# Half of the weight sums on GpSimd moved from the scan into the first products of layer 2, and the residual tiles' pools split anew

## The chip, the cores and the metric

The kernel runs on one core of a Trainium2 chip. The metric is the device time of the whole program in microseconds, median of several executions. Beside it there is one profiled execution, from which every duration below is taken. PE is TensorE, DVE is VectorE, ACT is ScalarE, POOL is GpSimd, SP is SyncE, whose queue issues most DMAs.

## What is computed

The input x is fp32, 1024 channels of 64 × 64 positions (1024 × 4096). Four layers are applied, each to a group-normalized copy, and each adds its result to x:

```python
x = x + L0_conv(gn(x))     # a scan convolution
x = x + W1 @ gn(x) + b1    # 1x1 convolution, 1024 -> 1024
x = x + L2_conv(gn(x))     # below
x = x + W3 @ gn(x) + b3    # 1x1 convolution, 1024 -> 1024
```

Layer 2, cut to what matters here:

```python
xz = silu(in_proj_w @ x + in_proj_b)          # 3072 x 4096
x_ssm, res, gate = split(xz, 3)               # WX, WR, WG below
xf = silu(depthwise_conv3(x_ssm) + dw_b)
perm = argsort(mobius_score)                  # an order of the 4096 tokens, for each of two heads
dt, B, C = split(dbc_w @ xf + dbc_b)          # 1 + 8 + 8 rows per head
y = selective_scan(xf[perm], softplus(dt)[perm], A, B[perm], C[perm], D)[inverse perm]
out = silu(out_proj_w @ (y * silu(gate) + res) + out_proj_b)   # WO below
```

## The kernel before, in words

**Matrices and products.** Six 1024 × 1024 matrices are multiplied with 1024 × 4096 data: W1, WX, WR, WG, WO, W3. W1, WX and WR run as a one-step fast product, 7 products of halves in place of 8 (`multiply`, L827, called by `run`, L898; columns go in four pairs of 512-column blocks). The right-hand sides of the seven are b21, b11, b22 and the combinations t1 to t4, made in `b_sets` (L786, the subtractions at L799 partly on DVE, partly on POOL) for the next pair while the present one is multiplied. WG, WO and W3 run at the end as a two-step product (`two_steps`, 7 × 7 = 49 products a job, 12 jobs); 9 of the 49 left-hand sides are blocks of the matrix, 40 are sums of blocks, which have to lie in DRAM (`s2_d`) before.

**The sums.** `sum_weights2` (L463) makes these 40 sums of one matrix, in chunks of `width` columns. A chunk loads 16 blocks into a tile of 7 × 4 × width per partition (four loads, L477), makes the inner sums with four POOL operations of 128 × 4·width (L479 and, inside `sub`, L470), stores three of the four block columns (L486), makes the outer sums in place with four POOL operations of 128 × 7·width (L490, L470), and stores four more (L497). Since the outer sums write over what the first stores read, they wait for these stores; the next chunk's loads wait for the last ones, as there is one tile. It is a generator: at each `yield` it hands over to the loop that advances it, and one advance is called a step here. Steps place the instructions in each engine's order; they are no waits in themselves.

**The stages.** Layer 0 takes the first 240 us, layer 1 up to 640. Sums for WR and WG are made in layer 1. From 640 to 1130 WX is multiplied (L1230 to L1262). For each output block the depthwise convolution follows, then turned rows are made: four 128-column pieces are turned on PE (L1086), copied by ACT (`l2xt`, three buffers, L1088), added into `acc` by POOL (L1094), and stored as token rows to `tok_d` by SP. `sort_on` advances the sort that gives `perm` in the same loop, by a written list of 14 numbers, one for each product of a pair.

From 1130 to 1645 the scan runs (L1302 to L1430) beside WR's products. An iteration k gathers the rows of the tokens of iteration k + 5 from `tok_d` in the order of perm (`gather`, L1310, an indirect DMA on POOL), turns rows (`turn_rows`, L1324 and L1325), makes the decay (DVE), `cross` (L1346), `weigh` (L1354 to L1359), `apply` (L1363), and scatters the result (`scatter`, L1372, also on POOL). `next_units` puts WR's products between. WR's results go through `rg` tiles: `put2b` (L1026) copies the first part out of PSUM by ACT, `add2b` adds the rest, `activate` applies silu and stores to `res_d`. Before the scan loop starts, `first` = 13 units of WR are put: eight beside the end of WX's stage, five after the first five gathers.

The same loop makes the sums for WO and then W3: one step an iteration, except where `given // 2 % 14 == 12`:

```python
sums = (None for m in (WO, W3) for _ in sum_weights2(m, ph, nc.sync, 64, lag=(1, None)))
...
                if given // 2 % 14 != 12:
                    next(sums, None)
```

With `lag=(1, None)` a chunk takes four steps: loads; two steps later the inner sums and, in the same step, the first stores; one step later the outer sums and the last stores; one step later the next chunk. Two matrices of eight chunks of width 64 make 64 steps.

**Pools.** `rg` tiles, one for each output block of a put, lie in two pools: `l2r` with four tiles, opened before WX's stage (L1017), and `l2r2` with six, opened after it in memory that WX's stage (`l2a` and its companions) has just left. The first six `rg` tiles of WR (for the products b21, b22 and t2) are made before `l2r2` is open, so all in `l2r`; from the seventh on (t3's first) the written rotation `[prg] * 6 + rg_pools * 4` holds, six tiles of `l2r2` and then four of `l2r`. `sort_pool` is on the right side of the memory and closes after WX's stage.

**Order.** In the loops concerned the order on DVE, PE, POOL and ACT is the written one (`manual_schedule`); SP's is that of the DMA calls.

Of the kernel before, what the change touches and what calls it, by code (L numbers as in the profile page):

```python
# [20 lines left out]
P = 128  # L21
# [73 lines left out]
def tile_net(ctx: ExitStack, tc: tile.TileContext, x, par_d, cst_d, w_d, w2_d, dbcw_d, out):  # L95
# [318 lines left out]
    def sort_on(quiet, n):  # L414


        while coming[0] is not None:
            was = coming[0]
            if was == "compare":
                if n == 0 or not quiet:  # L420
                    return
                n -= 1
            coming[0] = next(order, None)
            if was != "compare" or coming[0] != "compare":
                return
# [9 lines left out]
    def pause(n, first=None):  # L435
        yield first
        for _ in range(n - 1):
            yield
# [21 lines left out]
                dma.dma_start(d[:, at], w)  # L460
            yield

    def sum_weights2(m, pool, dma, width=P, lag=(0, 0)):  # L463

        eng = nc.gpsimd

        def sub(out, a, b):
            eng.tensor_tensor(out, a, b, ALU.subtract)  # L470

        for c in range(2 * QO // width):
            at = slice(c * width, (c + 1) * width)

            w = pool.tile([P, 7, 4, width], F32, tag="s2", name=f"s2_{m}_{c}", bufs=1)
            for i, block in ((0, 0), (1, 1), (2, 3), (5, 2)):
                dma.dma_start(w[:, i], w2_d[m - NW, 4 * block : 4 * block + 4, :, at].rearrange("j p e -> p j e"))  # L477
            yield from pause(1 + lag[0])
            eng.tensor_tensor(w[:, 3], w[:, 5], w[:, 2], ALU.add)  # L479
            sub(w[:, 5], w[:, 0], w[:, 5])  # L480
            sub(w[:, 4], w[:, 3], w[:, 0])
            sub(w[:, 6], w[:, 1], w[:, 4])
            if lag[1] is not None:
                yield from pause(1 + lag[1], True)
            for j, block in enumerate((0, 1, 3)):
                dma.dma_start(s2_d[m][3:, j, :, at].rearrange("i p e -> p i e"), w[:, 3:, block])  # L486
            if lag[1] is None:
                yield True
            a11, a12, a21, a22 = (w[:, :, j] for j in range(4))
            eng.tensor_tensor(a22, a21, a22, ALU.add)  # L490
            sub(a21, a11, a21)
            sub(a11, a22, a11)
            sub(a12, a12, a11)
            if lag[1] is not None:
                yield from pause(1 + lag[1], True)
            for j, v in ((3, a22), (4, a11), (5, a21), (6, a12)):
                dma.dma_start(s2_d[m][:, j, :, at].rearrange("i p e -> p i e"), v)  # L497
            yield

# [474 lines left out]
    def forget(pairs):  # L976
        for pair in pairs:
# [7 lines left out]
    norm2, last = {}, NP * NG * 7 - 1  # L985
    FIRST, SECOND = ([row * KH + g * OG + o for row in range(2) for o in range(OG)] for g in range(NG))
    sums = (busy for f in (sum_weights(WR, sum1, nc.scalar, lag=(1, 1)),
                               sum_weights2(WG, sum1, nc.scalar, lag=(2, 1))) for busy in f)
    with tc.manual_schedule(engines={E_.DVE, E_.PE, E_.Pool, E_.Activation}):
        for i, _ in enumerate(pointwise("l1", W1, "b1", [3, 2] + EARLY, x0_d, x1_d)):  # L990
            busy = next(sums, None) if i % 14 < 13 else None
# [22 lines left out]

    rg_pool = tc.tile_pool(name="l2r", bufs=4)  # L1017
    rg_pools = [rg_pool.__enter__()]
    part, silus = {}, []

    def put2b(m, o, nb, ps):
# [19 lines left out]
    with tc.tile_pool(name="l2a", bufs=2) as pa, tc.tile_pool(name="l2a2", bufs=1) as pa2, \  # L1041
# [184 lines left out]
        with tc.manual_schedule(engines={E_.DVE, E_.PE, E_.Pool, E_.Activation}):  # L1226
            nc.sync.dma_start(both[:, :, P:], dbcw_d)
            nc.gpsimd.tensor_copy(both[:, :, :P], ident.unsqueeze(1).to_broadcast([P, CT, P]))
            nc.gpsimd.memset(row, 0.0)
            ends, i, chain = iter(()), -1, None  # L1230
            for half in run(EARLY + LATE, [WX], normed(norm2), put2a, add2a, before2,
                            last_eng=nc.vector, fine=True, tell=True, begun=begun):
                if len(norm2) < CT:
                    n = len(SECOND)
                    if chain is None:
                        moments("gn2b", SECOND, range(2, 4), mv2)
                        chain = norm_steps("gn2b", mv2[:, 0, :n], mv2[:, 1, :n], n, finer=True)
                        turns = 0
                    turns += 1
                    if turns < 3:  # L1240
                        next(chain), next(chain)
                    else:
                        columns(SECOND, finish_of(chain), norm2)
                if half:
                    if coming[0] == "take":
                        sort_on(True, 0)
                    if due3:
                        turn(*due3.pop(0))
                elif half is False:
                    turned = bool(due3)  # L1250
                    follow()
                    follow_on()
                if half is not None:
                    continue
                i += 1
                if i > 14 and i % 14 == 4:
                    ends = finish(i // 14 - 1)
                next(ends, None)
                if coming[0] != "turn" or not turned:
                    sort_on(True, (0, 0, 0, 1, 3, 1, 0, 2, 0, 2, 3, 3, 0, 0)[i % 14])  # L1260
            while coming[0] is not None:
                sort_on(True, 1)  # L1262

            forget(EARLY)
            units = run([3, 2] + EARLY, [WR], normed(norm2), put2b, add2b, before2, fine=True, B=last_B[0])
            total, first, given = NP * 2 * NG * 7, 13, 0

            def next_units(upto):
                nonlocal given
                if given < upto:  # L1270
                    given += 1
                    next(units, None)

            while ready or due or due2 or due3:
                follow()
                next_units(8)
                next_units(8)
                follow_on()
                next_units(8)
                activate(len(silus))  # L1280
            spare = []
            for i in range(2):
                w = pa.tile([P, 2 + 2 * FB], F32, tag="xs", name=f"row{i}", bufs=4)[:, : 3 * HEADS * NF2]
                nc.gpsimd.memset(w, 0.0)
                spare.append(w.rearrange("p (b h c) -> p b h c", b=3, h=HEADS))
            for _ in finish(NP - 1):
                pass

    sort_pool.__exit__(None, None, None)

    with tc.tile_pool(name="l2g", bufs=8) as pgat, tc.tile_pool(name="l2b", bufs=2) as pb, tc.tile_pool(name="l2r2", bufs=6) as prg, tc.tile_pool(name="l2h", bufs=1) as ph, \
            tc.tile_pool(name="ps2b", bufs=1, space=PSUM) as psb:
        rg_pools[:] = [prg] * 6 + rg_pools * 4
        G2 = [ph.tile([P, P], F32, name=f"G{i}") for i in range(2)]
        B2 = [(ph.tile([MW, P], F32R, name=f"bts{i}"), ph.tile([MW, S, LC], F32R, name=f"cd{i}"))
              for i in range(2)]  # L1300
# [73 lines left out]
                in_=y, in_offset=None,  # L1374
            )

        sums = (None for m in (WO, W3) for _ in sum_weights2(m, ph, nc.sync, 64, lag=(1, None)))

# [461 lines left out]
```

## Time and profile before

| what | us |
|---|---|
| median of 3 executions | 2714.77 (2713.36 to 2717.06) |
| the profiled execution | 2715.32 |
| its span (first to last instruction) | 2713.4 |
| PE busy in the span | 2578.7 |
| POOL busy in the span | 1218.4 |
| layer 0, 0 to 240: PE busy | 163.43 |
| layer 1, 240 to 640: PE busy | 391.81 |
| scan stage, 1130 to 1645: PE, DVE, ACT, POOL busy | 485.95, 365.97, 330.00, 314.98 |

A span is what the profiler sees between the first and the last instruction; the time of the execution has 1.9 us around it. Where PE's clock column is below 1, its matmuls run slower though they count as busy. A hole before an instruction is put down to what released it last.

### The profile page before, as it was taken

The numbers are of one execution on the slowest core, as the hardware profiler recorded it, in microseconds if no ns is written. First come the engines' busy times: TensorE is split into PE (matmuls) and PEld (weight loads), VectorE is DVE, ScalarE is ACT, GpSimd is POOL, SyncE is SP. The second block draws the span as 40 slices with busy tenths as digits, with TensorE's granted clock in tenths as the row PEclk, the third lists the DMA queues.
The fourth block names the chain that finished last, engine by engine and source line by source line (L and its number), as shares of the span: only waits on it lengthen the run. The fifth ranks groups of instructions, "written<-read, shape, count | busy, mean of one in ns | idle before, by whom it ended". The sixth has DMA issues, their size and how long they took to land.

```text
span 2713.4 us, 30641 instructions
## 1 busy us (share of the span) xinstructions
PE 2578.7 (95%) x9520; PEld 1718.4 (63%) x9520; DVE 1817.8 (67%) x3870; ACT 1086.8 (40%) x1839; POOL 1218.4 (45%) x1100
## 2 busy tenths in 40 slices
PE   4788999999999999999999999999999999899999
PEld 3664444444555555444454447888888888788887
DVE  6996856655555644477677766577585676877777
ACT  4783110103656555476767554332243133311220
POOL 4154123232122120257575655576565566554544
PEclk9898999999999999999999999999999999999999
DMA  7245467546443373587877975889899898788896
GB/s 288 107 166 201 148 218 266 186 124 231 125 150 105 111 170 110 165 257 231 240 234 235 314 222 172 240 242 297 226 294 274 240 304 232 249 295 296 301 320 218
DMA packets 422741, 597.22 MB, mean 220 GB/s; under 512 B 141972, under 2 KB 210707, under 8 KB 419508
## 3 DMA queue, kind: packets, MB, share of 16 engines
q1 hardware_dynamic: 298020, 367.89, 42.4%
q10 hardware_dynamic: 91456, 136.33, 14.4%
q0 software_dynamic: 33104, 91.04, 13.1%
q8 instruction: 77, 1.26, 0.2%
q14 instruction: 84, 0.69, 0.1%
HBM read 435.10 MB, written 160.05 MB: 219 GB/s over the span
## 4 chain that ended last, share of the span: by engine, by line
PE 45%; DMA 6%; DVE 2%; ACT 2%; POOL 1%; SPq 1%; issue 1%; ACTq 0%; POOLq 0%; DVEq 0%
PE mm L841 7%; PE q_P6P L1716 5%; PE q_P5P L1716 5%; PE q_P7P L1716 5%; PE q_P4P L1716 5%; PE q_P2P L1716 5%; PE q_P3P L1716 5%; PE q_P1P L1716 4%; PE py L1363 1%; DMA s_d<-s 1%; DMA x_x_b<-x_d 1%; POOL s L470 1%; DMA s<-in_w_dram 1%; DMA g<-tok_d,src 1%; DMA x_x_Z<-x_d 1%
## 5 line engine op out<-in xcount | busy, mean ns | idle before, releaser
L841 PE MATMUL mm<-t,w 128*128 128x512 f32 x1536 | 694.4, 603 | 7.9 <-POOL t L799 4.1
L841 PE MATMUL mm<-b,w 128*128 128x512 f32 x1152 | 515.1, 598 | 4.0 <-ACT b L945 2.9
L841 PEld LDWEIGHTS mm<-t,w 128*128 128x128 f32 x1536 | 289.7, 193 | 337.0 <-issue 318.4
L841 PEld LDWEIGHTS mm<-b,w 128*128 128x128 f32 x1152 | 216.4, 192 | 253.0 <-issue 240.7
L1067 DVE SCALAR_TENSOR_TENSOR cvp<-xs,par,cvp 128x512 f32<-128x512 f32 x128 | 95.3, 754 | 75.5 <-ACT cvp L1064 73.3
L1685 ACT COPY qQ<-q_P5P 128x512 f32<-128x512 f32 x48 | 28.1, 586 | 293.7 <-PE q_P5P L1716 276.8
L1094 POOL TENSOR_TENSOR acc<-l2xt,acc 128x136 f32<-128x136 f32 x56 | 29.0, 519 | 235.5 <-ACT l2xt L1088 234.6
L470 POOL TENSOR_TENSOR s<-s 128x256 f32<-128x256 f32 (+3 forms) x120 | 130.1, 1091 | 7.9
L1118 DVE TENSOR_TENSOR xs<-mm,xs 128x512 f32<-128x512 f32 x64 | 41.8, 685 | 124.2 <-PE mm L841 124.2
L1366 ACT COPY g<-py 8x512 f32<-8x512 f32 x146 | 83.9, 574 | 95.0 <-PE py L1363 92.6
L960 DVE SCALAR_TENSOR_TENSOR image<-mm,par,image 128x512 f32<-128x512 f32 x64 | 47.0, 746 | 98.0 <-PE mm L841 98.0
L1372 POOL DMA_INDIRECT y_rows<-g,dst x74 | 73.5, 993 | 66.5 <-ACT g L1368 34.1
L1086 PEld LDWEIGHTS l2pt<-both,cv 128*128 128x128 f32 x512 | 76.5, 190 | 32.6 <-issue 23.9
L799 POOL TENSOR_TENSOR t<-t,b 128x512 f32<-128x512 f32 x40 | 56.0, 1425 | 91.2 <-DVE t L799 60.7
L1310 POOL DMA_INDIRECT g<-tok_d,src x74 | 72.1, 974 | 52.9 <-PE pr L1325 18.0
L1484 ACT ACTIVATE qb<-x_x_b,gn_bias,gn_r_r 128x512 f32<-128x512 f32 x64 | 48.8, 807 | 113.6 <-DMA wq_P4P<-s_d 32.3
L1354 DVE TENSOR_TENSOR E<-E,pg 128x512 f32<-128x512 f32 x74 | 50.5, 683 | 65.1 <-PE pg L1346 62.7
L945 ACT ACTIVATE b<-image,gnl_bias,gnl_r_r 128x512 f32<-128x512 f32 x48 | 37.2, 808 | 141.5 <-PE mm L841 69.2
L1716 PE MATMUL q_P4P<-t_t,wq_P4P 128*128 128x256 f32 x384 | 92.6, 385 | 1.3 <-DVE qV L1693 1.3
L1716 PE MATMUL q_P1P<-t_b,wq_P1P 128*128 128x256 f32 x384 | 92.3, 385 | 1.5 <-ACT qZ L1685 1.5
L799 POOL TENSOR_TENSOR t<-b,t 128x512 f32<-128x512 f32 x60 | 76.2, 1297 | 35.5 <-DVE t L799 35.3
L1480 POOL TENSOR_TENSOR t_t<-qt 128x512 f32<-128x512 f32 x23 | 29.6, 1289 | 137.6 <-DVE qt L1480 77.8
(419 smaller groups left out, 6037.6 us busy)
## 6 DMA issues: line engine op xcount, KB each, us to landing
w<-s_d SPq DMA_DIRECT2D x96, 512.0 KB, 3.7
w<-in_w_dram SPq DMA_DIRECT2D x72, 512.0 KB, 4.8
x_x_b<-x_d ACTq DMA_DIRECT2D x28, 1024.0 KB, 7.9
image<-x_d SPq DMA_DIRECT2D x12, 2048.0 KB
wq_P6P<-s_d SPq DMA_DIRECT2D x84, 256.0 KB, 4.7
wq_P7P<-s_d SPq DMA_DIRECT2D x84, 256.0 KB, 6.5
wq_P5P<-s_d SPq DMA_DIRECT2D x84, 256.0 KB, 3.0
wq_P3P<-s_d SPq DMA_DIRECT2D x84, 256.0 KB, 4.0
```

What stands on the lines that cost most here:

```text
L470: eng.tensor_tensor(out, a, b, ALU.subtract)
L799: eng.tensor_tensor(B[name][k], B[one][k], B[two][k], ALU.subtract)
L841: nc.tensor.matmul(to[o], w[:, k, o * P : (o + 1) * P], B[name][k], start=(fresh and k == 0), stop=(k == KH - 1), skip_group_check=True)
L960: nc.vector.scalar_tensor_tensor(part, ps, pcol(bias_name, o), part, ALU.add, ALU.add)
L1067: nc.vector.scalar_tensor_tensor(cv, xo[:, at + t : at + t + FB], pcol("dww", 3 * o + t), cv, ALU.mult, ALU.add)
L1086: nc.tensor.matmul(pt[:, q * NV : (q + 1) * NV], cv[:, (q0 + q) * P : (q0 + q + 1) * P], both[:, o, :], start=True, stop=True)
L1310: nc.gpsimd.indirect_dma_start(out=g[:, :], out_offset=None, in_=tok_d[:, :], in_offset=bass.IndirectOffsetOnAxis(ap=src[:, k : k + 1], ax ...
L1354: nc.vector.tensor_tensor(Ef, Ef, pg, ALU.mult)
L1366: nc.scalar.copy(rows[k + 1][h * LC : h * LC + S, :DH], py[h * LC : h * LC + S])
L1372: nc.gpsimd.indirect_dma_start(out=y_views[k % len(y_views)][:, :], out_offset=bass.IndirectOffsetOnAxis(ap=dst_[:, k : k + 1], axis=0), i ...
L1484: nc.scalar.activation(tile_of(j, name)[:, k], held[j, "x", name][:, k], AF.Identity, bias=bias, scale=scale)
L1716: nc.tensor.matmul(ps[:, o, :], w[:, k, o * P : (o + 1) * P], rhs[:, k, :], start=(new and o == 0 and k == 0), stop=(k == 1), skip_group_c ...
```

## The change

- `sum_weights2` takes five gaps in place of two lags: steps between loads and inner sums, inner sums and first stores, first stores and outer sums, outer sums and last stores, last stores and the next chunk. Its default equals what WG's sums had in layer 1. With `split` each group of four operations is cut in two by a further step.
- WO's sums are made in WX's stage: in a pool of their own (`sumx`, on the right side, one tile of 7 KB a partition), with gaps (2, 1, 1, 1, 1) and `split`, so eight steps a chunk and 64 in all. A step is taken in the slots where the sort's list has a zero, or in all of them when the sort is done, from the third on, and a second one at the half product that follows. What is left is done before WR's units start.
- W3's sums stay in the scan loop, alone, with gaps (2, 2, 1, 2, 1): eight chunks of eight steps, 64 steps as before. Inner sums and first stores are now two steps apart, outer sums and last stores too.
- The `rg` tiles: `l2r` has six tiles, and is opened on the right side once `sumx` and the sort's pool are closed; `l2r2` has four. The rotation from the seventh tile on becomes two of `l2r`, four of `l2r2`, four of `l2r`.

PE's and DVE's instructions keep their order; ACT's do but for one copy of an `rg` tile, which moves by two places.

```diff
--- before.py
+++ after.py
@@ -460,14 +460,16 @@
                 dma.dma_start(d[:, at], w)
             yield
 
-    def sum_weights2(m, pool, dma, width=P, lag=(0, 0)):
-
-
+    def sum_weights2(m, pool, dma, width=P, gaps=(3, 2, 0, 2, 1), split=False):
 
         eng = nc.gpsimd
 
         def sub(out, a, b):
             eng.tensor_tensor(out, a, b, ALU.subtract)
+
+        def rest(n, busy=None):
+            if n:
+                yield from pause(n, busy)
 
         for c in range(2 * QO // width):
             at = slice(c * width, (c + 1) * width)
@@ -475,27 +477,28 @@
             w = pool.tile([P, 7, 4, width], F32, tag="s2", name=f"s2_{m}_{c}", bufs=1)
             for i, block in ((0, 0), (1, 1), (2, 3), (5, 2)):
                 dma.dma_start(w[:, i], w2_d[m - NW, 4 * block : 4 * block + 4, :, at].rearrange("j p e -> p j e"))
-            yield from pause(1 + lag[0])
+            yield from rest(gaps[0])
             eng.tensor_tensor(w[:, 3], w[:, 5], w[:, 2], ALU.add)
             sub(w[:, 5], w[:, 0], w[:, 5])
+            if split:
+                yield True
             sub(w[:, 4], w[:, 3], w[:, 0])
             sub(w[:, 6], w[:, 1], w[:, 4])
-            if lag[1] is not None:
-                yield from pause(1 + lag[1], True)
+            yield from rest(gaps[1], True)
             for j, block in enumerate((0, 1, 3)):
                 dma.dma_start(s2_d[m][3:, j, :, at].rearrange("i p e -> p i e"), w[:, 3:, block])
-            if lag[1] is None:
-                yield True
+            yield from rest(gaps[2])
             a11, a12, a21, a22 = (w[:, :, j] for j in range(4))
             eng.tensor_tensor(a22, a21, a22, ALU.add)
             sub(a21, a11, a21)
+            if split:
+                yield True
             sub(a11, a22, a11)
             sub(a12, a12, a11)
-            if lag[1] is not None:
-                yield from pause(1 + lag[1], True)
+            yield from rest(gaps[3], True)
             for j, v in ((3, a22), (4, a11), (5, a21), (6, a12)):
                 dma.dma_start(s2_d[m][:, j, :, at].rearrange("i p e -> p i e"), v)
-            yield
+            yield from rest(gaps[4])
 
 
 
@@ -985,7 +988,7 @@
     norm2, last = {}, NP * NG * 7 - 1
     FIRST, SECOND = ([row * KH + g * OG + o for row in range(2) for o in range(OG)] for g in range(NG))
     sums = (busy for f in (sum_weights(WR, sum1, nc.scalar, lag=(1, 1)),
-                               sum_weights2(WG, sum1, nc.scalar, lag=(2, 1))) for busy in f)
+                               sum_weights2(WG, sum1, nc.scalar)) for busy in f)
     with tc.manual_schedule(engines={E_.DVE, E_.PE, E_.Pool, E_.Activation}):
         for i, _ in enumerate(pointwise("l1", W1, "b1", [3, 2] + EARLY, x0_d, x1_d)):
             busy = next(sums, None) if i % 14 < 13 else None
@@ -1014,8 +1017,9 @@
 
 
 
-    rg_pool = tc.tile_pool(name="l2r", bufs=4)
-    rg_pools = [rg_pool.__enter__()]
+    rg_pools = []
+    sumx_pool = tc.tile_pool(name="sumx", bufs=1, side="right")
+    sumx = sumx_pool.__enter__()
     part, silus = {}, []
 
     def put2b(m, o, nb, ps):
@@ -1227,7 +1231,8 @@
             nc.sync.dma_start(both[:, :, P:], dbcw_d)
             nc.gpsimd.tensor_copy(both[:, :, :P], ident.unsqueeze(1).to_broadcast([P, CT, P]))
             nc.gpsimd.memset(row, 0.0)
-            ends, i, chain = iter(()), -1, None
+            ends, i, chain, quiet = iter(()), -1, None, False
+            sums = sum_weights2(WO, sumx, nc.sync, 64, (2, 1, 1, 1, 1), split=True)
             for half in run(EARLY + LATE, [WX], normed(norm2), put2a, add2a, before2,
                             last_eng=nc.vector, fine=True, tell=True, begun=begun):
                 if len(norm2) < CT:
@@ -1246,6 +1251,8 @@
                         sort_on(True, 0)
                     if due3:
                         turn(*due3.pop(0))
+                    if quiet:
+                        next(sums, None)
                 elif half is False:
                     turned = bool(due3)
                     follow()
@@ -1256,10 +1263,20 @@
                 if i > 14 and i % 14 == 4:
                     ends = finish(i // 14 - 1)
                 next(ends, None)
+                some = (0, 0, 0, 1, 3, 1, 0, 2, 0, 2, 3, 3, 0, 0)[i % 14]
                 if coming[0] != "turn" or not turned:
-                    sort_on(True, (0, 0, 0, 1, 3, 1, 0, 2, 0, 2, 3, 3, 0, 0)[i % 14])
+                    sort_on(True, some)
+                quiet = i > 1 and (some == 0 or coming[0] is None)
+                if quiet:
+                    next(sums, None)
             while coming[0] is not None:
                 sort_on(True, 1)
+            for _ in sums:
+                pass
+            sumx_pool.__exit__(None, None, None)
+            sort_pool.__exit__(None, None, None)
+            rg_pool = tc.tile_pool(name="l2r", bufs=6, side="right")
+            rg_pools.append(rg_pool.__enter__())
 
             forget(EARLY)
             units = run([3, 2] + EARLY, [WR], normed(norm2), put2b, add2b, before2, fine=True, B=last_B[0])
@@ -1286,15 +1303,9 @@
             for _ in finish(NP - 1):
                 pass
 
-    sort_pool.__exit__(None, None, None)
-
-
-
-
-
-    with tc.tile_pool(name="l2g", bufs=8) as pgat, tc.tile_pool(name="l2b", bufs=2) as pb, tc.tile_pool(name="l2r2", bufs=6) as prg, tc.tile_pool(name="l2h", bufs=1) as ph, \
+    with tc.tile_pool(name="l2g", bufs=8) as pgat, tc.tile_pool(name="l2b", bufs=2) as pb, tc.tile_pool(name="l2r2", bufs=4) as prg, tc.tile_pool(name="l2h", bufs=1) as ph, \
             tc.tile_pool(name="ps2b", bufs=1, space=PSUM) as psb:
-        rg_pools[:] = [prg] * 6 + rg_pools * 4
+        rg_pools[:] = rg_pools * 2 + [prg] * 4 + rg_pools * 4
         G2 = [ph.tile([P, P], F32, name=f"G{i}") for i in range(2)]
         B2 = [(ph.tile([MW, P], F32R, name=f"bts{i}"), ph.tile([MW, S, LC], F32R, name=f"cd{i}"))
               for i in range(2)]
@@ -1374,7 +1385,7 @@
                 in_=y, in_offset=None,
             )
 
-        sums = (None for m in (WO, W3) for _ in sum_weights2(m, ph, nc.sync, 64, lag=(1, None)))
+        sums = (None for _ in sum_weights2(W3, ph, nc.sync, 64, (2, 2, 1, 2, 1)))
 
 
 
```

## The prediction

> **What bounds the kernel now.** I read the page first (busy shares and 40 slices), then the kernel cut into its stages, then PE's own timeline with the waits that open its holes, then the timelines of the engines named there.
>
> ```profile
> PE 2578.7 (95%) x9520; PEld 1718.4 (63%) x9520; DVE 1817.8 (67%) x3870; ACT 1086.8 (40%) x1839; POOL 1218.4 (45%) x1100
> 640.00:1130.00 490.00, 486.48 (x1498) 252.94 (x1497) 250.07 (x796) 266.85 (x476) 88.21 (x109) 1.00 0.46 136
> 1130.00:1645.00 515.00, 485.95 (x1335) 241.31 (x1334) 365.97 (x814) 330.00 (x570) 314.98 (x325) 0.98 0.79 244
> 1645.00:2345.00 700.00, 697.98 (x3359) 614.05 (x3358) 475.11 (x656) 207.19 (x325) 429.03 (x324) 1.00 0.88 256
> ```
>
> The stage rows give start:end, length, busy time of PE, PEld, DVE, ACT and POOL, granted clock, DMA share, GB/s. TensorE is the bound: 95% of the whole, and the first third of layer 2 (640 to 1130, WX's products) has only 3.5 us of 490 to give. The scan stage (1130 to 1645, WR's products beside the scan) is the one that leaks: 29 us of holes, and at a clock of 0.98 another 12 us (below). It is also where POOL is busy 315 us, against 88 in the stage before. The change moves POOL and DMA work from the second to the first. PE's work stays the same, so the change can win or lose only holes and the clock that follows them. PE's timeline shows the large ones (start, busy, [hole before <- what ended it]), and four windows show the clock around them:
>
> ```profile
> 1136.92 5.40 PE L841 MATMUL mm<-t,w 128*128 128x512 f32 x8 [3.73 <-ACT rg L1026]
> 1326.00 0.98 PE L1324 MATMUL pr<-cst,g 128*128 128x192 f32 x2 [4.02 <-DMA g<-tok_d,src]
> 1539.61 3.67 PE L841 MATMUL mm<-t,w 128*128 128x512 f32 x4 [3.19 <-POOL t L799]
> 1612.13 0.98 PE L1324 MATMUL pr<-cst,g 128*128 128x192 f32 x2 [5.14 <-DMA g<-tok_d,src]
> 1133.00:1143.00 10.00, 5.70 (x10) 2.19 (x10) 1.98 (x3) 5.26 (x8) 5.53 (x10) 0.83 0.61 152
> 1321.00:1333.00 12.00, 7.98 (x16) 3.91 (x15) 4.62 (x11) 6.52 (x12) 5.61 (x7) 0.72 1.05 297
> 1536.00:1545.00 9.00, 5.81 (x13) 2.71 (x13) 3.16 (x10) 1.41 (x4) 6.26 (x7) 0.81 1.05 373
> 1606.00:1620.00 14.00, 8.86 (x18) 4.21 (x16) 4.90 (x12) 3.70 (x8) 4.83 (x5) 0.76 0.79 256
> ```
>
> Length times (1 − clock) is time lost to the clock: 1.7, 3.4, 1.7 and 3.4 us. I call the four A, B, D, F; C is one at 1487 (2.8 us behind G on DVE, 1.7 of clock); E one of 0.91 us at 1561, again t from POOL.
>
> Why B and F? Gathers are issued five iterations ahead, yet the data comes late. POOL's timeline just before each (same columns) and its waits over 1140 to 1640 (total, times, longest):
>
> ```profile
> 1313.48 1.13 POOL L490 TENSOR_TENSOR s<-s 128x448 f32<-128x448 f32 x1 [3.20 <-DMA s_d<-s]
> 1314.69 3.57 POOL L470 TENSOR_TENSOR s<-s 128x448 f32<-128x448 f32 x3
> 1318.40 0.98 POOL L1310 DMA_INDIRECT g<-tok_d,src  x1
> ...
> 1599.76 1.12 POOL L490 TENSOR_TENSOR s<-s 128x448 f32<-128x448 f32 x1 [3.03 <-DMA s_d<-s]
> 1600.96 3.56 POOL L470 TENSOR_TENSOR s<-s 128x448 f32<-128x448 f32 x3
> 1604.67 0.98 POOL L1310 DMA_INDIRECT g<-tok_d,src  x1
> POOL s L490 <- DMA s_d<-s: 48.4, 15, 6.5
> POOL s L479 <- DMA s<-in_w_dram: 18.0, 5, 4.1
> ```
>
> POOL stands behind the sums' own stores and loads, and the gather stands behind POOL. The reader is to see that the 67 us of waiting cost as much as half the arithmetic: before, a chunk's second group of sums is handed out one step after its first stores, and the stores need longer than that.
>
> [...] 3.4 us are lost behind each hole of 4 to 5 us, 1.7 us behind those of 2.8 to 3.7. [...] Here two such subtractions (L799) took 2.64 us at C beside the sums and 1.28 at 1349, where POOL was free. [...]
>
> **The change part by part.**
>
> *Sums of WO leave the scan.* Sixteen chunks of 4 × 0.735 + 4 × 1.13 = 7.5 us make 119 us of POOL there, with 67 of waiting 186 of some 500 us. Eight chunks leave, some 93 us. The remaining eight get two steps instead of none between first sums and stores, so three instead of one between first and second sums. A step is one iteration, about 6.5 us (74 in some 490), so the stores, which hold POOL up by 6.5 us at most, are mostly in when the second sums come. Gains, hole plus clock: B 4.02 + 3.4 = 7.4, F 5.14 + 3.4 = 8.5. POOL was over 20 us late there; a small lag eats none of the five-iteration lead. I take 0.9 of B, 0.85 of F: 6.7 + 7.3. D, 3.19 + 1.7 = 4.9: t3's second pair on POOL came after 3.0 us of sums and a gather, in an order that stays, though other chunks now stand there; 0.65, so 3.2. E 0.6 of 0.9 = 0.55. C: G waits on a DVE chain slowed by POOL; the extra 1.36 us and the clock are some 3 us, of which 0.4 = 1.1. Sum 18.8. DMA falls by 14.3 MB of 126 (8 × (512 KB loads + 1280 KB stores)); no weight wait appears among PE's, so this gains nothing.
>
> *Same sums in WX's stage.* 61 us of POOL on top of 88 in 490; DMA 66.6 to 81 MB. Behind the sums on POOL stand 64 acc additions of 0.52 us (L1094), which free xt (three buffers, any three turns take 10.4 us or more), and t3/t4; on SP, 5.7 us a chunk of issues (7 loads and 4 stores, from SP's gaps) stand before tok_d stores and weights. With splitting, the longest uninterrupted group is 2 × 1.13 us, and a store awaited adds up to 6.5. POOL may be 10 us late there, SP some 6. The stage's PE waits are 3.5 us in all, so there is cover. If it is gone, each group costs its overhang. Bounds −0.5 (PE has next to nothing to gain here) to +24 (below); I take +1, with 6 as the range's end.
>
> *Pools split 6 and 4.* The seventh rg tile (t3's first put, the copy that opens A) was the first in l2r2, in memory under WX's pools, and waited for all of these to empty. Now it takes l2r's first tile again and waits for that tile's store alone, issued near 1108. But A is not simply 3.73 + 1.7 us of gain. The gathers' chain does not move: last turn 1119.8, tok_d stores 1130, memset of G 1136.35 after 5.05 us of waiting for them, first gather 1138.09, needed by turn_rows, data in near 1142.4. PE has 13 units to do first, of which the 36 matmuls left at A make 36 × 0.436 = 15.7 us. PE starts those 3.7 us earlier, ends them at 1136.9 instead of 1142.3 (the clock loss inside included), and waits about 5.5 us for the gather: one hole for another, and past 4 us the clock loss becomes 3.4 for 1.7. Hole +1.8, clock +1.7, less the 0.57 us that already stood there: +2.7, from −1 (the gathers start earlier because SP and POOL are emptier) to +3.5. A new wait: the very first rg copy (1091.6) now takes memory of the sort and of WO's sums, so waits for their last stores; behind it in ACT's queue stand l2xt's copies, for which PE's turns wait. Those stores are issued well before, so nothing, or their 6.5 us at most.
>
> *New waits in the scan.* SP's and POOL's orders change: stores later by two steps, at t3 a pair of 128x448 sums between the halves. A hole appearing elsewhere: bound 0 to 5 (one like D), take 1.5. At the turn into two_steps the last sums end at the same step as before; 0.3, from −1 to +3.
>
> Sum: −18.8 + 2.7 + 1 + 1.5 + 0.3 = −13.3. On the profiled execution's own 2715.32 us (span 2713.4, 1.9 around it) that is 2702.0; the runs' median is 0.55 lower, so 2701.5.
>
> **Rivals.**
> - *Only part goes.* Iteration gather, cross, weigh and apply is a chain over DVE, PE and ACT too; C stays whole, D and E too as t3's order is unchanged, and half of B and F move elsewhere. Then 18.8 falls to about 9, less costs of 4 to 5: −5, so 2710. For it: G and ds holes exist that no sums explain. Against: B and F follow POOL's queue directly.
> - *All goes.* B to F with their clock leave whole (7.4 + 8.5 + 4.9 + 0.9 + 4.5 = 26.2) and A costs nothing more, WX 1.5: −25, so 2690. For it: the sums were 186 us of POOL; against: A's gather chain is fixed.
> - *The first third becomes POOL-bound (slower).* Place: L1094 behind the pairs of 128x448 and behind awaited stores; xt stays taken, ACT's copy waits, then PE's turn. Price: 16 such pairs × 1.5 us = 24, less a gain without WX of 14.3: +9.7, so 2724. It decides from 0.9 us of PE time per pair, 1.2 for slower beyond 0.2%. For it: stores there were waited on up to 6.5 us. Against: POOL idle 350 us in acc's waits for ACT, DMA at 0.46.
>
> **How the numbers follow.** About 0.2% (5.4 us) is what a measurement can tell from no change: faster is below 2709.3, slower above 2720.2. Forecast 0.53 (its own range 2694 to 2711), only part 0.21, all 0.12, slower 0.14. Most of the forecast, all of "all goes" and half of "only part" are faster: 0.51 + 0.12 + 0.11 = 0.74. The rest of these, 0.12, is the same; slower 0.14. The range 2689 to 2714 leaves out a third of "all goes" (0.04), a little of "only part" (0.02) and the slower case: 0.2.
>
> **What would show it.** Right: no hole of gathers over 3 us in the scan stage, its clock at 0.99, POOL's waits on s_d under 15 us, PE's busy share of 640 to 1130 still 99%; and near 1137 a hole of 5 to 6 us ended by the gather where the rg wait was. Wrong: POOL or ACT l2xt holes in WX's stage, tok_d stores landing later, t3 or G holes unchanged in number, or new holes at weights (w) behind SP's later stores. If the gather at A is already in when PE gets there, I was too dear by 2.7 us or more.

## The result

The median fell to 2698.76 us (2695.57 to 2701.45, six runs) beside 2714.98 for the kernel before on the same chip: a ratio of 0.9937, 95% interval 0.9924 to 0.995. The profiled execution took 2699.02 us, with a span of 2696.9. The forecast was 2701.5.

The two stages that the change touches, in the kernel after (same columns as in the prediction; the scan's stage now ends at 1630):

```profile
640.00:1130.00 490.00, 483.81 (x1490) 251.14 (x1489) 256.24 (x780) 266.95 (x478) 146.08 (x171) 1.00 0.60 164
1130.00:1630.00 500.00, 478.70 (x1337) 238.24 (x1336) 367.19 (x830) 326.60 (x566) 256.84 (x261) 0.99 0.70 223
```

POOL has 146 us in WX's stage for 88 before, and 257 in the scan for 315. TensorE is busy 483.8 of 490 us in WX's stage, 2.7 less than before: that is a price. In the scan all large holes but one have gone, and with them the slow clock behind them (0.99 granted, for 0.98 before). PE's waits from 630 to 1660 of the kernel after (total, times, longest) name what is left:

```profile
PE pr L1335 <- ACT ds L1329: 9.4, 1, 9.4
PE py L1374 <- DVE G L1370: 4.7, 4, 1.4
PE pr L1336 <- ACT ds L1329: 3.5, 4, 0.9
PE l2pt L1090 <- ACT l2xt L1092: 2.9, 4, 1.4
```

Gathers (9.2 us in two waits before) and t (4.1) are off the list, and the G wait of 2.8 us is down to 1.4. In their place stands one hole of 9.4 us, and l2xt waits that were 0.3 us. On POOL, from 1140 to 1630, no wait for the sums' loads or stores is among the nine longest (66 us before); what POOL waits for now is results of the scan's own chain:

```profile
POOL y_rows L1383 <- ACT g L1379: 166.6, 49, 7.9
```

PE executes the same instructions in the same order in both kernels, so the two can be laid side by side at the same instruction. This table, from the start times in the two traces, is the account of the gain (us):

| from, to | before | after | difference |
|---|---|---|---|
| start, to WX's first turn (l2pt) | 660.6 | 660.0 | −0.6 |
| WX's first turn, to the last dbc product of its end (end_dbc) | 461.0 | 464.5 | +3.5 |
| A: from there to 40 matmuls past the scan's first turn (pr) | 34.6 | 40.3 | +5.7 |
| the rest of the scan, to the first two-step product | 485.8 | 463.4 | −22.4 |
| two-step products | 1064.5 | 1061.5 | −3.0 |

Place A in the kernel after, on PE, POOL and ACT:

```profile
1124.63 14.86 PE L844 MATMUL mm<-t,w 128*128 128x512 f32 x34
1148.86 0.98 PE L1335 MATMUL pr<-cst,g 128*128 128x192 f32 x2 [9.38 <-ACT ds L1329]
```

```profile
1140.14 0.34 POOL L1313 MEMSET G<- 128x128 f32 x2 [5.44 <-DMA tok_d<-row]
...
1141.88 1.08 POOL L1321 DMA_INDIRECT g<-tok_d,src  x1 [0.18 <-issue]
```

```profile
1148.51 0.35 ACT L1329 ACTIVATE ds<-cst,g 128x64 f32<-128x64 f32 x1 [9.75 <-DMA s<-in_w_dram]
```

PE now runs 34 matmuls in one piece, where the rg wait cut them before, and is out of work at 1139.5. The first gather is issued at 1141.88, and ACT can make ds from it only at 1148.5. The name that the view gives for ACT's wait is that of a load which landed last; ds reads g, and nothing of s. The trace has the gather landed at 1148.13, 6.2 us after its issue (4.2 in the kernel before). From there to 1148.46 ACT works off four more semaphore waits ahead of ds. The kernel before has a list of that kind at its rg copy (done at 1136.24), and its ds waits for the gather alone: the wait at the rg tile has in part moved to ds, where it costs 0.4 us. The clock's record has half speed from 1143.8 to 1154.0, so 5.2 us of it after the hole: another 2.6 us.

### The profile page after: what moved, and what is told of

It is laid out like the page before. It is cut to its first block, busy times and chain, and to the rows that moved or that the text cites. A ratio compares the mean times of both kernels' runs of the same rounds, so it can differ in the third digit from the quotient of the medians.

```text
span 2696.9 us, 30618 instructions
## 1 busy us (share of the span) xinstructions
PE 2568.1 (95%) x9520; PEld 1714.4 (64%) x9520; DVE 1833.7 (68%) x3870; ACT 1084.6 (40%) x1839; POOL 1217.9 (45%) x1100
## 3 DMA queue, kind: packets, MB, share of 16 engines
q0 software_dynamic: 33104, 91.04, 13.3%
## 4 chain that ended last, share of the span: by engine, by line
PE 79%; DVE 10%; ACT 7%; DMA 2%; issue 1%; SPq 0%; POOL 0%; DVEq 0%; ACTq 0%; POOLq 0%
PE mm L844 36%; PE q_P6P L1727 5%; PE q_P5P L1727 5%; PE q_P7P L1727 5%; PE q_P2P L1727 5%; PE q_P4P L1727 5%; PE q_P3P L1727 5%; PE q_P1P L1727 5%; PE l2pt L1090 2%; PE py L1374 2%; DVE xt L632 1%; DVE cvp L1071 1%; DVE stats L554 1%; ACT b L948 1%; ACT xt L598 1%
## 5 line engine op out<-in xcount | busy, mean ns | idle before, releaser
L844 PE MATMUL mm<-t,w 128*128 128x512 f32 x1536 | 686.1, 598 | 0.0
L1704 DVE TENSOR_TENSOR qV<-q_P4P,qV 128x512 f32<-128x512 f32 x96 | 64.9, 687 | 38.6 <-PE q_P4P L1727 37.0
L1727 PE MATMUL q_P5P<-t_t,wq_P5P 128*128 128x256 f32 x384 | 90.8, 379 | 0.0
L1727 PE MATMUL q_P6P<-t_t,wq_P6P 128*128 128x256 f32 x384 | 90.7, 379 | 0.0
```

The lines of the kernel that those rows point to most:

```text
L844: nc.tensor.matmul(to[o], w[:, k, o * P : (o + 1) * P], B[name][k], start=(fresh and k == 0), stop=(k == KH - 1), skip_group_check=True)
L1704: nc.vector.tensor_tensor(to, ps, to, ALU.add)
L1727: nc.tensor.matmul(ps[:, o, :], w[:, k, o * P : (o + 1) * P], rhs[:, k, :], start=(new and o == 0 and k == 0), stop=(k == 1), skip_group_c ...
```

## The experiments

All ratios are to the kernel before, run on the same chip in the same session. The table gives the stretches of the table above for each profile; A and the rest of the scan are one column, because some experiments move work between them.

| kernel | ratio (95% interval) | WX | A and scan | two-step |
|---|---|---|---|---|
| before | 1 | 461.0 | 520.4 | 1064.5 |
| after | 0.9937 (0.9924 to 0.995) | 464.5 | 503.6 | 1061.5 |
| e1, pools alone | 1.0016 (1.0007 to 1.0025) | 462.7 | 524.0 | 1063.0 |
| e2, rg wait restored | 0.9926 (0.9909 to 0.9943) | 464.0 | 498.6 | 1060.5 |
| e3, no sums for WO | 0.9931 (0.9914 to 0.9947) | 461.0 | 502.6 | 1061.2 |
| e4, 19 units first | 0.9911 (0.9894 to 0.9927) | 465.3 | 493.5 | 1060.5 |
| e5, tight gaps for W3 | 0.9944 (0.9924 to 0.9964) | 463.9 | 503.2 | 1061.8 |
| e6, rg stores later | 0.9936 (0.9915 to 0.9958) | 466.7 | 501.7 | 1060.6 |
| e7, groups of four uncut | 0.9939 (0.9918 to 0.996) | 463.2 | 502.1 | 1063.3 |
| e8, e4 and loads on ACT | 0.9968 (0.996 to 0.9977) | 476.0 | 493.5 | 1059.6 |
| e9, e4 and e7 | 0.99 (0.9885 to 0.9915) | 463.3 | 495.2 | 1060.5 |
| e10, e1 and 19 units first | 0.995 (0.9933 to 0.9968) | 461.0 | 514.2 | 1061.4 |

**e1: the pools' part alone.** From the kernel before:

```diff
-    rg_pool = tc.tile_pool(name="l2r", bufs=4)
-    rg_pools = [rg_pool.__enter__()]
+    rg_pools = []
...
+            sort_pool.__exit__(None, None, None)
+            rg_pool = tc.tile_pool(name="l2r", bufs=6, side="right")
+            rg_pools.append(rg_pool.__enter__())
...
-tc.tile_pool(name="l2r2", bufs=6) as prg
+tc.tile_pool(name="l2r2", bufs=4) as prg
-        rg_pools[:] = [prg] * 6 + rg_pools * 4
+        rg_pools[:] = rg_pools * 2 + [prg] * 4 + rg_pools * 4
```

> The kernel before with the pools' part alone (l2r six tiles opened after WX, l2r2 four, the new rotation); all sums stay in the scan. Theory (one hole for another): near 1137 the rg wait of 3.7 us is gone, but PE then waits for the first gather, 5 to 6 us with the clock at half for 6.8 us; loss at A some 9 us against 6.0 before, and the later holes (gathers near 1326 and 1612, t near 1539) stay. Time 2 to 4 us over before: about 2718. Rival (the pools win, and the loss at A in the changed kernel comes from the sums): A loses at most 3 us, time about 2710.

Measured: 1.0016, slower by 0.07 to 0.25%. In e1's PE timeline the rg wait is gone, and this stands there:

```profile
1146.15 0.98 PE L1320 MATMUL pr<-cst,g 128*128 128x192 f32 x2 [8.19 <-ACT ds L1314]
```

A takes 38.9 us for 34.6, the rest of the scan 485.2 for 485.8. So the pools' part on its own costs 4.3 us at A and gives nothing elsewhere: the theory's trade, dearer than the 5 to 6 us of hole it named. The rival is out: no sum was moved here.

**e2: the rg wait restored in the kernel after.** The pools stay as in the kernel after. Only the rotation is changed, so that the seventh tile lies under WX's pools again:

```diff
-        rg_pools[:] = rg_pools * 2 + [prg] * 4 + rg_pools * 4
+        rg_pools[:] = [prg] * 4 + rg_pools * 6
```

> The changed kernel with the four l2r2 tiles first in the rotation, so that the seventh rg tile waits again for the memory under WX's pools. Theory: the hole of 9.4 us that the first gather ends is cut in two or replaced by one of 3 to 4 us at the rg copy, the clock loss falls from 5.1 to under 3.4 us, and the time is 3 to 6 us below the changed kernel: about 2694. Rival (the pools' part is a gain in the new place): the rg hole comes on top of the gather's, time 3 to 6 us above the changed kernel: about 2703.

Measured: 0.9926, in profile 5.1 us less at A than the kernel after (and 3.3 less than e6, which has the least of the others with this pools' part and 13 units), with the rest of the scan at 463.4 as in the kernel after. On PE:

```profile
1139.65 5.40 PE L844 MATMUL mm<-t,w 128*128 128x512 f32 x8 [4.21 <-ACT rg L1030]
1145.67 0.56 PE L1335 MATMUL pr<-cst,g 128*128 128x192 f32 x2 [0.62 <-PE mm L844]
```

The wait put back makes the kernel faster in the trace. The medians' intervals overlap with the kernel after's, so the 5 us rest on the profile, on e1's similar difference with the other sign, and on the mechanism. Two things do it. The half clock (3.4 us) now runs out under the eight matmuls ahead of the gather (5.40 us, for 3.65 at full speed at 1146.24), where PE has time. And the gather lands sooner: ds, which reads it, starts 4.2 us after its issue in e2 (issued at 1140.82) and in the kernel before (1138.09), against 6.6 us in the kernel after. ACT's ds in e2, then in the kernel before:

```profile
1145.07 0.35 ACT L1329 ACTIVATE ds<-cst,g 128x64 f32<-128x64 f32 x1 [1.12 <-DMA g<-tok_d,src]
1142.29 0.35 ACT L1318 ACTIVATE ds<-cst,g 128x64 f32<-128x64 f32 x1 [1.07 <-DMA g<-tok_d,src]
```

The rg wait also holds back the silus and the stores of four rg tiles, until 1.3 us after the gather's issue; without it, SP issues these 1 MB between 1140.4 and 1143.5, among the loads of W3's sums and around the gather's issue. What that order costs is tried in e6.

**e3: no sums for WO.** From the kernel after:

```diff
-            sums = sum_weights2(WO, sumx, nc.sync, 64, (2, 1, 1, 1, 1), split=True)
+            sums = iter(())
-            for _ in sums:
-                pass
...
-                d = s2_d[m][a, b]
+                d = s2_d[WG if m == WO else m][a, b]
```

> The changed kernel without WO's sums (the WO products read WG's sums instead, so that part of the output is not out_proj's). Theory: WX's stage ends 2.8 to 3.4 us earlier, since its l2xt waits (2.9 us) go, and the hole at A stays at 9 us or so, as the gathers hang on WX's last turn: about 2695.5. Rival (the sums also delay the gathers' chain): the hole at A falls to 6 us or less too, time about 2690. Second rival (the l2xt waits have another cause): time as the changed kernel, 2698.8.

Measured: 0.9931. WX's stage is back at 461.0 and its l2xt waits are off the list; A's hole is 8.3 us, the rest of the scan 463.4. So the sums cost WX's stage 3.5 us. A takes 39.2 us here, and 38.7 to 40.3 with the sums (after, e5, e7), so no part of A's loss is shown to be theirs: it is the pools' part. The first theory holds.

**e4: 19 units before the first turn.** From the kernel after:

```diff
-            total, first, given = NP * 2 * NG * 7, 13, 0
+            total, first, given = NP * 2 * NG * 7, 19, 0
```

> The changed kernel with 19 of WR's half products put before the scan's first turn instead of 13, 6 x 1.74 = 10.5 us more matmul work at the place where PE waits 9.4 us for the first gather. Theory: that hole and its clock loss of 5.1 us go, the 125 instead of 131 units left still fill the 76 iterations; time about 14 us below the changed kernel: 2685. Rival (the scan needs these units): the wait moves to later gathers or G, new holes of 1 to 3 us with clock loss; gain under 5 us, about 2695.

Measured: 0.9911. PE in e4:

```profile
1145.01 17.33 PE L844 MATMUL mm<-b,w 128*128 128x512 f32 x40
1162.18 0.49 PE L1335 MATMUL pr<-cst,g 128*128 128x192 f32 x2
```

There is no hole, and the clock stays at full speed through the whole scan (1.00 from 1130 to 1630). A and scan together fall by 10.1 us in the profile (the ratios put the whole gain at about 7), not by 14: the theory had added all 5.1 us of the clock's loss to the hole, but half of the slow time lies inside the hole and costs nothing. 9.4 + 2.6 = 12.0 could be had, and 1.1 of it went to a ds wait at 1172 and 0.3 to holes in the scan, which the theory had none of.

**e5: tight gaps for W3.** From the kernel after:

```diff
-        sums = (None for _ in sum_weights2(W3, ph, nc.sync, 64, (2, 2, 1, 2, 1)))
+        sums = (None for _ in sum_weights2(W3, ph, nc.sync, 64, (2, 0, 1, 0, 5)))
```

> The changed kernel with W3's gaps (2, 0, 1, 0, 5): the same 8 steps a chunk, but first stores in the step of the inner sums and last stores in that of the outer sums, as before. Theory (the moved half of the sums is what frees POOL): at one chunk in eight steps POOL has time to wait 6.5 us for a chunk's stores; no hole of gathers over 1 us, POOL's waits on s_d some 24 us, scan stage within 2 us of 463; time about 2699 to 2701. Rival (the wider gaps are what counts): POOL waits again at each chunk just ahead of the gathers, one or two holes of 3 to 5 us with clock loss return, scan stage 470 or more, time about 2708.

Measured: 0.9944, the rest of the scan 463.3, none of the old holes. POOL's wait from 1140 to 1630 is back:

```profile
POOL s L492 <- DMA s_d<-s: 20.8, 8, 5.3
```

That is 2.6 us a chunk, for 3.2 with sixteen (48.4 us in 15 waits), and no hole on PE comes of it: POOL catches up before the next gather is due. So it is moving half of the sums away that frees POOL; with that done, the wider spread of W3's is worth nothing on PE. What the spread would do with all sums in the scan was not tried.

**e6: rg stores later.** From the kernel after:

```diff
             while given < first:
                 next_units(total)
-                if len(silus) > 3:
-                    activate(4)
```

> The changed kernel without the activate call in the loop that puts the units before the scan's first turn, so that the silus and stores of four rg tiles (1 MB) come an iteration later, behind the first gathers. Theory (these stores delay the first gather): from issue to landing it takes about 4.8 us as in the kernel before, not 6.6; the hole falls from 9.4 to some 7.5 us and the loss with the clock by 2 to 3 us: about 2696. Rival (the gather takes its 6.6 us for another reason, such as the loads of W3's sums): hole and time as in the changed kernel, 2698.8 or some 1 us more for a table load.

Measured: 0.9936. From the gather's issue at 1142.42 to ds at 1148.23 it takes 5.8 us, between the two. A falls by 1.9 us to 38.4, with a hole of 7.6 us, as foreseen, though the slow clock behind it costs 2.4 us for 2.6; WX's stage took 2.2 us more in this execution, 1.7 of it at a half clock behind a hole at 911, so the time can't be told from the kernel after's. The table load that the rival names takes 1.28 us on ACT (at 1152.34). The expectation set 4.8 us to PE's read beside 6.6 to ds; from ds to ds, 4.2 is what was to be reached. SP's queue in e6 suggests why it was not:

```profile
1140.48 2.03 SPq L479 DMA_DIRECT2D s<-in_w_dram  x4
1142.56 13.02 SPq L827 DMA_DIRECT2D w<-s_d  x2
1155.62 2.35 SPq L1042 DMA_DIRECT2D res_d<-rg  x4
```

A load of weights (512 KB) moved up to the place of the stores, 0.1 us behind the gather's issue. The four loads of sums stand ahead of the gather by about as much as in e2 and in the kernel before (0.4 us for 0.3). That the stores delay it is shown for 0.8 us of 2.4; that the load of weights makes up the rest is what the order suggests, and was not tried alone.

**e7: groups of four uncut.** From the kernel after:

```diff
-            sums = sum_weights2(WO, sumx, nc.sync, 64, (2, 1, 1, 1, 1), split=True)
+            sums = sum_weights2(WO, sumx, nc.sync, 64, (2, 2, 1, 2, 1))
```

> The changed kernel with WO's groups of four POOL operations not cut in two (gaps 2, 2, 1, 2, 1): each stands as 2.9 or 4.6 us in one piece before acc's additions, DMAs at the same steps. Theory (WX's 3.5 us loss comes from SP's queue, where loads and stores of the sums stand before the stores that free l2xt): WX's stage within 1 us of the changed kernel's 464.5, time 2699. Rival (POOL's groups hold acc and with it l2xt): more and longer l2xt waits, stage 468 or more, time 2703 or more.

Measured: 0.9939; WX's stage 463.2. Groups of up to 4.6 us of POOL in one piece don't make the stage longer, so the rival, POOL's groups holding acc, is out. Two other paths show in the kernel after, with 2.6 of the 3.5 us (PE's waits near 1000 and at 1044). The first is SP (SP's queue, then ACT, then PE):

```profile
986.06 2.02 SPq L479 DMA_DIRECT2D s<-in_w_dram  x4
...
989.15 0.58 SPq L1104 DMA_DIRECT2D tok_d<-l2xt  x1
```

```profile
999.02 0.76 ACT L1092 COPY l2xt<-l2pt 128x324 f32<-128x324 f32 x2 [4.84 <-DMA tok_d<-l2xt]
```

```profile
999.50 1.37 PE L1090 MATMUL l2pt<-both,cv 128*128 128x162 f32 x8 [1.41 <-ACT l2xt L1092]
```

By the trace's semaphores, ACT's copy waited for the store issued at 989.15. The tile had been copied by 983.96, so the store stood 5.2 us behind loads of sums, weights and the image; it landed at 998.92, 9.8 us after its issue. In the kernel before the same store was issued as soon as its tile was copied, and landed after 5.5 us:

```profile
983.54 0.37 SPq L1100 DMA_DIRECT2D tok_d<-l2xt  x1
```

So SP's queue makes about half of the delay, and the time in flight the other half. With WO's sums on SP the store is 3.6 to 5.2 us late and 9.6 to 10.4 in flight (after, e2, e4 to e7, e9), without these sums 0 and 4.3 to 5.5 (before, e1, e3, e10). What PE waits for it changes from one execution to the next: 0 to 1.9 us in the five kernels with the same WX stage (after, e2, e4, e5, e6). The second path is DVE, and is told in the last section; its wait is 1.0 to 1.9 us in these five, and absent in e7.

**e8: loads of WO's sums on ACT's queue, with 19 units.** From e4:

```diff
-                dma.dma_start(w[:, i], w2_d[m - NW, ...
+                (nc.scalar if m == WO else dma).dma_start(w[:, i], w2_d[m - NW, ...
```

> The 19 half products, and the loads of WO's sums issued on ACT's queue instead of SP's; their stores stay on SP. Theory (SP's queue makes WX's loss): about half of the 2.9 us of l2xt waits go, WX's stage falls to about 463, time 1 to 2 us below the kernel with 19 alone: 2687. Rival (ACT pays for the issues and for waiting for the last chunk's stores): ACT's copies of l2xt come later, WX's stage 468 or more, time 2692 or more.

Measured: 0.9968, the rival, and about 15 us worse than e4 by the ratios. The profiled execution is e8's fastest, 2694.48, so the others lose more than its trace shows. On ACT:

```profile
987.58 4.32 ACTq L479 DMA_DIRECT2D s<-in_w_dram  x4
991.94 0.76 ACT L1092 COPY l2xt<-l2pt 128x324 f32<-128x324 f32 x2 [5.70 <-DMA w<-s_d]
```

ACT did nothing from 986.2 to 991.9, with the four loads at the head of its queue, and the copy behind them came late; PE waited 5.4 us, and the clock fell for 6.8. The l2xt store of e7's account is now issued as soon as its tile is copied and lands after 7.1 us, so the loads' move did clear SP's queue; since ACT loses more by it, what SP's queue alone costs PE stays untested. This is the mechanism of the prediction's slower rival, a ring of l2xt held by work queued ahead, and in this form it costs 11 us of WX's stage.

**e9: 19 units and uncut groups.** From the kernel after, the edits of e4 and e7 together:

```diff
-            sums = sum_weights2(WO, sumx, nc.sync, 64, (2, 1, 1, 1, 1), split=True)
+            sums = sum_weights2(WO, sumx, nc.sync, 64, (2, 2, 1, 2, 1))
-            total, first, given = NP * 2 * NG * 7, 13, 0
+            total, first, given = NP * 2 * NG * 7, 19, 0
```

> The 19 half products together with WO's groups in one piece, the two edits that took time off one by one. Theory (both act in different stages, so they add): WX's stage at 463 to 464, the hole at A gone, the scan from the first turn on as in the kernel with 19 alone; ratio to the kernel before 0.990, about 2688. Rival (the 1 to 2 us of the uncut groups were chance of one execution): ratio as with 19 alone, 0.991 or above.

Measured: 0.99 (2688.62 beside 2715.76), the WX stage at 463.3, no hole at A. It has the lowest ratio of all, faster than before by 0.85 to 1.15%; against e4 the intervals overlap, so that the second edit adds anything is read from the WX stage alone. The scan took 1.7 us more than in e4: a half clock of 3.4 us at 1209.8, behind a hole of 2.3 us that e4 has too, without the slow clock.

**e10: pools' part and 19 units, sums in the scan.** From e1:

```diff
-            total, first, given = NP * 2 * NG * 7, 13, 0
+            total, first, given = NP * 2 * NG * 7, 19, 0
```

> The kernel before with the pools' part and 19 half products ahead of the first turn; all sums stay in the scan. Theory (A and the scan's holes are separate accounts): the hole of 8.2 us at A goes with its clock, some 10 us less than the pools alone, and B, D and F stay: ratio to the kernel before about 0.998, 2707. Rival (with fewer units left over for the scan and POOL still behind, the later holes grow by as much): ratio 1.0016 or above, as the pools alone.

Measured: 0.995, better than foreseen. A and scan fall by 9.8 us from e1, as the theory says, and holes with the sums as cause stay, at other places. POOL's waits, then PE's, in e10:

```profile
POOL s L490 <- DMA s_d<-s: 50.4, 16, 5.4
```

```profile
PE mm L841 <- POOL t L799: 7.2, 2, 6.4
PE pr L1320 <- DMA g<-tok_d,src: 4.0, 2, 3.5
```

Against e4, with all else equal, the sums' move is worth 514.2 − 493.5 = 20.7 us in the scan, less 4.3 in WX's stage: 16.4 in the profiles, about 11 by the ratios. Beyond the 9.8 us, the profiles of e1 and e10 differ in stretches that neither edit touches (WX 1.7, two-step 1.6). The ratios are 18 us apart, for 13 in the profiles; that remainder is not explained.

## Why the prediction came out right

**The sum.** −13.3 was foreseen. The three stretches that the prediction argued about made −22.4 + 5.7 + 3.5 = −13.2. The total of the profile, −16.5 in the span, has some 3.3 more, nearly all from stretches whose order the change leaves alone; the two-step products took 1059.6 to 1063.3 us in all the experiments and 1064.5 only in the profile of before, and the cause of that stays open. The direction and the cause were right. That the sum agrees so closely is luck: the gains, 17.3 foreseen with "new waits in the scan" taken off, were 5.1 too small, and the costs of A and of WX's stage, 3.7 foreseen, were 5.5 too small.

**Gains in the scan, 18.8 less 1.5 for "new waits in the scan" foreseen, 22.4 measured.** The mechanism was right: POOL behind its queue, gathers and t behind POOL. e5 shows that the moved half carries it, and e3 that WO's sums, made elsewhere or not at all, leave the scan the same 463.4 us. The mis-sized term is the list of shares (0.9, 0.85, 0.65, 0.6, 0.4): everything that stood behind POOL went whole. Its clock part was too dear, in turn: time lost to the clock was counted over all the slow time, though slow time inside a hole costs nothing. Counted from the end of each hole, by the clock's record: B 4.0 + 2.8, F 5.1 + 3.1, D 3.2 + 1.7, E 0.9, C 1.4 + 1.7, together 23.9; less two small holes that came (G at 1499, 0.91; ds at 1559, 0.87) 22.1, for the 22.4 measured.

**D and the order of t3.** A share of 0.65 was given since the order around t3 stays. It went whole: that a sum stands ahead of t3 in the queue doesn't count once POOL reaches it in time.

**A, +2.7 foreseen, +5.7 measured.** The trade of one hole for another was right, and e1 and e2 show it from both sides. The step that failed is "data in near 1142.4": the gather's landing was taken over from the trace of before, where the very wait that goes had kept the stores of four rg tiles behind it. In the new order it took 6.2 us to land for 4.2, was issued 0.9 us later after WX's end (that time differs by up to 1.2 us from run to run, with no pattern by edit), and ds came 0.4 us after its landing. So PE waited 9.4 us and not 5.5. The clock, taken as 1.7 more, came to 2.6 for 1.7, so 0.9 more. Two figures of the working are also off: A has 34 matmuls left and not 36, and 1.8 + 1.7 − 0.57 is 2.9 and not 2.7.

**WX's stage, +1 taken, −0.5 to +24 as bounds, +3.5 measured.** The cover foreseen (POOL 10 us late without harm) held, and e7 shows it even for uncut groups. What wasn't covered was the l2xt store of 989, for which PE waited near 1000, and DVE at 1044. That SP's queue would hold such stores up was named in the prediction but taken as covered (a chunk has four loads and seven stores, not seven and four), and that they would be in flight for longer was not thought of; the second, DVE beside POOL's sums, was priced as a gain in the scan (C) and forgotten as a cost in the stage to which the sums went. ACT's l2xt holes in WX's stage were among the signs of being wrong that the prediction listed: they came, but small.

**The spread of W3's chunks.** The prediction had it make the stores "mostly in when the second sums come". It does (no wait for s_d left among POOL's longest), and with half of the sums moved it is worth nothing on PE, as e5 shows.

**How long the stores take.** POOL waits up to 6.5 us for the sums' stores in the kernel before; what makes them take so long is not shown. WG's sums in layer 1 are 128 columns wide, those of the scan 64. In the trace of before, the median landing of WG's last stores (448 KB) is 6.1 us, that of the scan's (224 KB) 2.5 us. Width, size, queue and traffic all differ between the two.

**The rivals.** "All goes" was nearest in the scan. "The first third becomes POOL-bound" did not happen through POOL; the ring of l2xt that it named is real, as e7's account and e8 show from SP's and ACT's side.

## What to carry to other kernels

When a wait is to go, ask first when the data that is needed next will be there, and which transfers the old wait had kept apart from it: here removing one cost 4 to 5 us, and six more units of work in its place won 10 in the profiles. Work moved off POOL's queue gave back every large hole behind it whole here (22.4 us in the scan), once the queue had slack; in the stage it goes to, look at all the queues that its loads and stores join, at how long other stores are then in flight (9.6 to 10.4 us here, for 4.3 to 5.5), and at the engine whose operations run beside it. Count clock loss only from the end of a hole (2.6 us of 5.1 at A).

## What was not expected of the hardware

Small DVE operations took five times as long beside POOL's sums (1.01 us for 0.19, 1.20 for 0.23). DVE in the kernel after, while POOL ran four 128x448 sums from 1028.28 to 1033.04, then the same operations in the kernel before, where POOL was free:

```profile
1028.45 1.01 DVE L1188 TENSOR_SCALAR row<-acc 128x64 int32<-128x64 int32 x1
1029.49 1.20 DVE L1190 TENSOR_TENSOR row<-acc,row 128x64 f32<-128x64 f32 x1
```

```profile
1026.85 0.19 DVE L1184 TENSOR_SCALAR row<-acc 128x64 int32<-128x64 int32 x1
1027.08 0.23 DVE L1186 TENSOR_TENSOR row<-acc,row 128x64 f32<-128x64 f32 x1
```

Three operations of 0.2 us took about as long as the sum beside each (1.13 us), and ended within 0.1 us of it. Not every one does: a TENSOR_SCALAR of the same shape took 0.18 us at 1030.62, between two sums, and xs took 1.28 us for two beside the last sum, as in the kernel before. From the operation on acc ahead of these to xs it is 3.8 us for 1.1; cv and l2xt on ACT came late by as much, and PE waited 1.04 us at 1044. Why the two engines' operations end together is not shown.

A hole of 1.8 us at 911 (a sort's product behind DVE's swap) is in every profile, and the clock fell behind it for 3.4 us in e1 and in e6 alone; in the kernels before and after it did not. The hole of 2.3 us in e4 and e9 is another such case. So a hole shorter than the slow time (1.8 or 2.3 us beside 3.4) cost clock in one execution and none in the next, and the length of a hole alone, which the prediction set beside the loss, does not tell it.
